# Layer 0 of a four-layer graph network: gathers three parts ahead instead of eight, ranks on ScalarE, early projections one part apart, last norms on ScalarE

## The chip, the cores and the metric

The kernel runs on one core of a Trainium2 chip. The metric is the time of one execution on the device, in microseconds (us). The engines are named as in the profile: PE (TensorE, matrix products), PEld (its weight loads), DVE (VectorE), ACT (ScalarE), POOL (GpSimd) and SP (SyncE, which here only issues DMAs). Each engine works through its own instructions in a fixed order and waits where an instruction needs the result, or the buffer, of another engine.

## The reference, cut to what matters

The input is a matrix x of 3327 nodes with 256 features and an adjacency matrix adj (int32, symmetric, about 1% ones, ones on the diagonal). Four graph attention layers follow one another, each with a residual and a layer norm:

```python
x = layernorm(x + L0(x, adj, ...))   # one head, score = a . leaky_relu(g_src[i] + g_tgt[j])
x = layernorm(x + L1(x, adj, ...))   # one head, score = leaky_relu(s1[i] + s2[j])
x = layernorm(x + L2(x, adj, ...))   # one head, score = s_src[i] + s_dst[j]
x = layernorm(x + L3(x, adj, ...))   # two passes of four heads of 64, leaky_relu, elu
return x
```

In each, a node's scores over its neighbours go through a softmax, and the weighted sum of the neighbours' projected rows is the layer's output. In layer 0 the leaky_relu is taken of a vector of 256 for every pair of neighbours, so it has no cheap product form. Layers 1 to 3 need only an outer sum of two columns.

## The kernel before, in words

The 3327 rows are 26 tiles of 128. **Layer 0 (sparse0)** works on the neighbours alone. The tiles form four groups of 4, 7, 9 and 6 tiles (SETS). For each group, `neighbours` finds the neighbours of its rows from the adjacency matrix: SP loads pieces of 1024 columns, ACT converts them to bf16 and counts the ones (`convert`, L543), PE adds column numbers, DVE takes the largest eight of each chunk (`scan`, L579), sorts them (`sort`) and writes them down (`note`, L599 and L606). Each row then gets a key from its number of neighbours (`turn_key`: ACT, PE, ACT), and its rank among the rows of the group is the number of keys above its own: one DVE operation per tile that compares all key rows of the group with the tile's keys and counts them (L678), then a conversion to integers, ranks_i (L682). With the ranks the rows are sorted by degree: POOL writes each tile's list of neighbours to its place (`write_list`, L731, one indirect DMA per tile), and reads the sorted lists back (`read_lists`, L739). Sorted tiles hold rows of like degree, so that a tile t gathers only as many neighbours as its largest row has (LEVELS), between 26 and 56.

The gathers of a tile are cut into **parts** of up to four neighbours, 237 parts in all; the groups begin at parts 0, 39, 102 and 182. For a part, POOL issues one indirect DMA per neighbour (`gather`, L912); each fetches 128 rows, one per partition, into one of 22 buffers g of four rows (TURNS). Before the first part of a tile, `gather_own` (L897) fetches the tile's own rows into one of four buffers. DVE scores the part (`score`: L932 takes the larger of two vectors for all four neighbours at once, L938 multiplies by the attention vector and adds up, once per neighbour). At a tile's last part DVE takes the largest score and ACT makes the weights. From the next step on ACT multiplies each gathered row by its weight (`combine`, L1012), and PE adds the rows up in PSUM (L1015). For the very last tile, all rows but those of four cuts are added on DVE instead (`add_aside`, L991 and L993). `add_input` (L1041, L1045, L1048, on DVE) divides by the sum of the weights and adds the residual, ten steps after the tile's last part, and `put_back` (L1057, on POOL) writes the tile's result to its unsorted place in DRAM. When a group is complete, `take` loads its rows back (DMAs issued by ACT), `finish_sums` makes means and variances on DVE, `finish_root` takes the root on POOL (L1097), and `finish` normalizes on DVE (L1106).

The order of the work of layer 0 is written out by hand. A loop over the parts q, called steps, does for each q: some units of `neighbours` of the next group, as many as are needed to have that group done by its due step (`owed`; `steps_of` says how many units a group has); then whatever is noted for step q (`due`, filled by `at_step`); then `gather(q + LEAD)`, with the gathers of own rows noted for it (`once_placed`); then `score(q)`. So LEAD, 8 parts, says how far POOL's gathers stand ahead in program order of the scores and of everything else that is noted for a step. `put_back` and `write_list` are appended to a list `between` and issued one after every second gather. The due step of a group's lists is its begin less LEAD, 2 and half its size and 1: with respect to POOL's gathers, `write_list` and `read_lists` stand at the same place for any LEAD, since the gathers move by LEAD too. Each engine's own queue holds only its own instructions, in this order; so between engines LEAD shows only where one waits for another.

Beside the gathers the projections of layer 1 for the first three groups are done early, tile by tile (`turn_next`, `project_next`, L1142 to L1170), one tile every two steps; those of the third group (group 2) begin 38 steps after the last group's first part, or later. They run through PE, ACT and stores on SP (L1160), and the last one ends with the rates of a block of tiles (L1164 to L1170).

**Layers 1 to 3** are dense: for each block of columns (7, 7, 6 and 6 tiles) a loop runs over the 26 source tiles j. DVE (layers 1 and 3) makes the unnormalized weights e of j by one operation per head (`weigh`, L1629), and PE multiplies them into accumulators (L1723, L1773, L1781). Layer 1 begins with what is left of layer 0: the last group's `take`, sums, root and norms (`last_group`) are worked off inside its first loop. Layer 3 is two such passes of four heads. What comes after a block is put in a list of pending work, and is worked off, a piece per j, inside the next block's loop. For the second pass that is `finish_last` (its `add` at L1947 to L1953): back to rows, elu, residual, moments, then `scaled` (L250 adds the epsilon on DVE, L251 takes the root on POOL, L257 normalizes tile by tile on DVE), then SP stores the rows to the output. After the last block this work stands at the kernel's end. `scaled` is also what `norms` calls in the other layers.

Of the kernel before, what the change touches and what calls it, by code (L numbers as in the profile page):

```python
# [8 lines left out]
F32 = mybir.dt.float32  # L9
# [10 lines left out]
P = 128  # L20
# [30 lines left out]
def gat_stack(  # L51
# [226 lines left out]
    def sparse0(lost):  # L278
        GROUP, TURNS, LEAD, SPREAD = 4, 22, 8, 8
        starts = [sum(SETS[:s]) for s in range(len(SETS))]  # L280
        with ExitStack() as s0:
# [238 lines left out]
            def steps_of(s):  # L520
                return SETS[s] * (len(banks_n) + 2) + 8

            def neighbours(s):
# [151 lines left out]
                yield  # L675
                for t in range(size):
                    junk = find.tile([P, max(SETS) * P], U16, tag="junk_r", name="junk2", bufs=1)
                    nc.vector.tensor_scalar(  # L678
                        junk[:, : size * P], key_rows[:, : size * P], keys[:, t : t + 1], 0.0,
                        op0=ALU.is_gt, op1=ALU.add, accum_out=ranks[:, t : t + 1],  # L680
                    )
                nc.vector.tensor_copy(ranks_i[:, :size], ranks[:, :size])  # L682
                placed[s] = ranks_i, payloads
# [547 lines left out]
            for q, key in ends.items():  # L1231
# [9 lines left out]
                if key[1] == SETS[key[0]] - 1 and key[0] < len(SETS) - 1:  # L1241
                    at_step(q + 21, take, key[0])
                    at_step(q + 27, finish_sums, key[0])
                    at_step(q + 33, finish_root, key[0])
                    at_step(q + 37, finish, key[0])
            for s, q in begins.items():
                work, at = excess(s), max(q - 2, 0)
                for y in range(12):
                    at_step(at + y, go_on, work)
# [4 lines left out]
            for s in range(len(SETS) - 1):  # L1254
                for it in range(starts[s], starts[s] + SETS[s]):
                    at_step(at, turn_next, it)
                    at_step(at + 2, project_next, it)
                    at += 2
                if s == len(SETS) - 3:
                    at = max(at, begins[len(SETS) - 1] + 38)  # L1260
            def keep_targets(s):
# [244 lines left out]
    def layers(rs, early=0, rest=None):  # L1506
# [402 lines left out]
        def finish_last(b, o, sums):  # L1909
# [45 lines left out]
            yield from staged([(s, s) for s in range(len(block))], [(0, back), (3, add)])  # L1955
            yield from scaled(block, [h[it] for it in block], mv)
            for it in block:
# [182 lines left out]
```

## Time and profile before

| What | Value |
| --- | --- |
| Time, median of 5 runs | 2954.26 us (2949.02 to 2961.05) |
| Profiled execution: time, span | 2954.82 us, 2953.0 us |
| Busy share of the span | PE 79%, DVE 72%, PEld 46%, POOL 34%, ACT 28% |
| Instructions | PE 15862, DVE 5634, ACT 2358, POOL 1061 |
| Mean granted clock of PE | 0.873 |
| Gathers (L912, POOL) | 894, 853.0 us busy, 954 ns each |
| First to last gather | about 86 to 1343 us |
| First matmul of layer 1 | 1365.85 us |
| Ranks (L678, DVE) | 26, 29.8 us busy, median 1146 ns |

The spans of the table are those of one profiled execution; the times of the profile's rows begin at the start of its span. A row of a group gives the line, the engine, the operation, the tensors (out<-in), the count, then the busy time in us and the mean in ns of one, then the idle time of the engine ahead of the group and what ended most of it. A row of a timeline gives the start in us, the busy time, and in brackets the idle time just before with its releaser. A row of waits gives the engine and line that waited, for which engine's result, and then the total in us, the number of times and the longest.

### The profile page before, as it was taken

The page shows a single profiled execution, that of the slowest core. Times are in us where ns is not written, and L with a number is a line of the kernel's source. Part 1 is how long each engine was busy: PE and PEld are TensorE (multiplying, and loading weights), DVE is VectorE, ACT ScalarE, POOL GpSimd, SP SyncE. Part 2 cuts the span into 40 slices and gives each one's busy share as a digit, 9 for nine tenths or more (in the row PEclk, how much of TensorE's full clock was granted, in tenths as well). Part 3 has the DMA queues.
Part 4 walks back from the last instruction along what each step waited for, and adds up shares of the span by engine and source line. Part 5 has one row for each costly group of instructions (what it writes and reads, how often), then busy time and mean ns, then how long its engine had stood idle before and what let it go on. Part 6 is the DMA issues. An engine that isn't in the chain of part 4 may idle for free. (4 is left out here: it accounts for less than half of the span.)

```text
span 2953.0 us, 45075 instructions
## 1 busy us (share of the span) xinstructions
PE 2318.7 (79%) x15862; PEld 1357.3 (46%) x15862; DVE 2140.2 (72%) x5634; ACT 840.6 (28%) x2358; POOL 994.1 (34%) x1061
## 2 busy tenths in 40 slices
PE   7466767556545416647899999999999999999997
PEld 4222323222222103325788888863556667534332
DVE  6789789968776528765455521138999999899997
ACT  4244445434334304543344311111010110110111
POOL 2676767777777777772000000000000000000000
PEclk8576777777767757889999999999999999999998
DMA  7684655445644435545766633331222222212211
GB/s 236 201 264 145 187 167 165 140 132 156 166 112 114 112 107 124 171 121 171 226 208 195 196 82 111 106 96 45 77 60 82 75 79 64 71 45 59 59 45 48
DMA packets 183854, 370.50 MB, mean 125 GB/s; under 512 B 35772, under 2 KB 124707, under 8 KB 182596
## 3 DMA queue, kind: packets, MB, share of 16 engines
q1 hardware_dynamic: 103994, 178.49, 21.0%
q0 software_dynamic: 51008, 155.70, 18.8%
q10 hardware_dynamic: 28618, 33.33, 3.2%
q8 instruction: 128, 2.10, 0.3%
q14 instruction: 106, 0.87, 0.1%
HBM read 327.52 MB, written 46.23 MB: 127 GB/s over the span
## 5 line engine op out<-in xcount | busy, mean ns | idle before, releaser
L912 POOL DMA_INDIRECT g<-table_d,lst x894 | 853.0, 954 | 273.0 <-issue 247.1
L1629 DVE SCALAR_TENSOR_TENSOR e<-rate,feat,at 128x896 f32<-128x896 f32 (+4 forms) x832 | 843.1, 1078 | 58.1 <-PE acc L1781 47.3
L1015 PE MATMUL acc<-g,ident 128*128 128x512 f32 (+1 forms) x896 | 505.5, 708 | 265.1 <-ACT g L1012 247.7
L1773 PE MATMUL acc<-e,feat 128*32 128x384 f32 (+2 forms) x6656 | 697.2, 515 | 6.4 <-DVE h L1745 3.4
L1773 PEld LDWEIGHTS acc<-e,feat 128*32 128x32 f32 x6656 | 307.0, 110 | 304.7 <-issue 159.0
L1015 PEld LDWEIGHTS acc<-g,ident 128*128 128x128 f32 x896 | 195.2, 228 | 483.3 <-ACT g L1012 365.6
L1781 PE MATMUL acc<-e,feat 128*32 128x384 f32 (+3 forms) x3328 | 383.2, 512 | 0.0
L1012 ACT ACTIVATE g<-g,w 128x256 f32<-128x256 f32 x883 | 365.5, 495 | 0.4 <-ACT minus L489 0.4
L932 DVE TENSOR_TENSOR y<-g,minus_ps 128x1028 f32<-128x1028 f32 (+2 forms) x233 | 273.2, 1173 | 126.4 <-DMA g<-table_d,lst 119.0
L938 DVE SCALAR_TENSOR_TENSOR y<-y,a_ps 128x257 f32<-128x257 f32 x894 | 324.5, 418 | 25.1 <-PE a_ps L781 5.8
L1723 PE MATMUL acc<-feat,e 128*128 128x257 f32 (+2 forms) x1352 | 303.9, 382 | 8.3 <-DVE inv L1744 5.7
L251 POOL TENSOR_TENSOR rstds<-rstds,minus_half 128x7 f32<-128x7 f32 (+1 forms) x12 | 19.7, 1643 | 773.9 <-DVE rstds L250 773.9
L1723 PEld LDWEIGHTS acc<-feat,e 128*128 128x128 f32 (+2 forms) x1352 | 254.9, 191 | 46.5 <-issue 8.6
L1723 PE MATMUL acc<-feat,at 128*128 128x257 bf16 (+2 forms) x2028 | 237.8, 274 | 4.1 <-DMA at<-at_d 3.9
L1781 PEld LDWEIGHTS acc<-e,feat 128*32 128x32 f32 (+1 forms) x3328 | 161.9, 110 | 130.7 <-issue 87.9
L1723 PEld LDWEIGHTS <-at 128*128 128x128 bf16 (+2 forms) x2028 | 198.8, 99 | 37.9 <-DMA at<-at_d 4.4
L553 PE MATMUL v<-code,leads 65*128 65x512 bf16 (+1 forms) x182 | 82.7, 456 | 155.7 <-DVE cand L579 121.9
L1629 DVE SCALAR_TENSOR_TENSOR e<-rate,feat,at_i 128x896 f32<-128x896 f32 (+2 forms) x104 | 112.2, 1080 | 90.8 <-DMA at_i<-in_adj_t_dram 43.1
L579 DVE MAX8 cand<-v 128x8 f32<-128x104 f32 (+2 forms) x858 | 158.6, 259 | 20.8 <-PE v L556 20.8
L1609 POOL DMA_DIRECT2D rate3b_d<-rate_rows x4 | 2.1, 520 | 450.5 <-ACT rate_rows L1608 450.5
L1656 ACT CAST at<-at_i 128x896 bf16<-128x896 int32 (+2 forms) x104 | 92.1, 885 | 112.5 <-DMA at_i<-in_adj_t_dram 75.6
L553 PEld LDWEIGHTS <-leads 65*128 65x128 bf16 x182 | 22.1, 121 | 191.1 <-DVE cand L579 161.2
(248 smaller groups left out, 1832.2 us busy)
## 6 DMA issues: line engine op xcount, KB each, us to landing
adj_i<-in_adj_dram SPq DMA_DIRECT2D x75, 512.0 KB
at<-at_d SPq DMA_DIRECT2D x150, 224.0 KB
at_i<-in_adj_t_dram SPq DMA_DIRECT2D x50, 448.0 KB
at<-at_d SPq DMA_DIRECT2D x75, 192.0 KB
at<-at_d SPq DMA_DIRECT2D x75, 191.8 KB
g<-table_d,lst POOLq DMA_INDIRECT x894, 2.8
at_d<-at ACTq DMA_DIRECT2D x50, 224.0 KB
at_i<-in_adj_t_dram SPq DMA_DIRECT2D x25, 384.0 KB
```

The lines of the kernel that those rows point to most:

```text
L553: nc.tensor.matmul(v[:, :w], leads[:, b, :], code[:, :w], start=True, stop=False)
L579: nc.vector.max(spread[:, c0 + c, :], view(v[:, :w]))
L912: nc.gpsimd.indirect_dma_start(out=g[:, k - k0, :], out_offset=None, in_=table_d[:, :], in_offset=bass.IndirectOffsetOnAxis(ap=entry["lst" ...
L932: nc.vector.tensor_tensor(y, rows, minus_src[:, None, :].to_broadcast([P, m, dim + 1]), op=ALU.max)
L938: nc.vector.scalar_tensor_tensor(y, y, 1.0, a_ps[:, : dim + 1], op0=ALU.mult, op1=ALU.mult, accum_out=sc)
L1012: nc.scalar.activation(rows, rows, AF.Copy, scale=w[:, k : k + 1])
L1015: nc.tensor.matmul(dst, ident, rows, start=start, stop=stop)
L1629: nc.vector.scalar_tensor_tensor(e[:pn, : c1 - c0], self.rate[b][:pn, h_of, : c1 - c0], q, at[:pn, : c1 - c0], op0=ALU.max, op1=ALU.mult,)
L1656: nc.scalar.copy(at[:pn, :w], at_i[:pn, :w])
L1723: nc.tensor.matmul(accs[s][:pn, : dim + 1], a[:pj, s * P : s * P + pn], f[:pj, : dim + 1], start=(j == 0 and part == 0), stop=(j == nt - 1 ...
L1773: nc.tensor.matmul(accs[x][p][q : q + 32, : hi - lo], f[:pj, at0 : at0 + 32], es[at0 // hd][:pj, lo:hi], start=(j == 0), stop=(j == nt - 1),)
L1781: nc.tensor.matmul(accs[x][pairs][h_of * 32 : (h_of + 1) * 32, : hi - lo], f[:pj, dim + h_of : dim + h_of + 1].to_broadcast([pj, 32]), es[ ...
```

## The change

Six things change. LEAD is 3 instead of 8. The later steps of a finished group come nearer to its last part: `take` after 17 steps instead of 21, `finish_sums` 21 instead of 27, `finish_root` 24 instead of 33, `finish` 27 instead of 37; the work on rows with more neighbours than seats (`excess`) begins one step before the group instead of two. The ranks of groups 1 to 3 are made by ACT: the sign of (key row minus key plus a half), added up, two tiles per unit of `neighbours`, and one DVE operation turns the sums into integers; `steps_of` counts these units. The buffer of the compared rows is bf16 there. Group 0's ranks stay on DVE. The early projections of group 2 stand one step apart instead of two, and begin 28 steps after the last group's first part instead of 38. In `finish_last`, the norms are done by ACT, as scale and shift, with one more DVE operation per block for the shifts; in the last block every second tile's norm stays on DVE. After the change, LEAD being 3, a group's lists are due five steps later in the order than before, `add_input` still stands ten steps after the tile's last part, and `put_back` thirteen.

```diff
--- before.py
+++ after.py
@@ -276,7 +276,7 @@
 
 
     def sparse0(lost):
-        GROUP, TURNS, LEAD, SPREAD = 4, 22, 8, 8
+        GROUP, TURNS, LEAD, SPREAD = 4, 22, 3, 8
         starts = [sum(SETS[:s]) for s in range(len(SETS))]
         with ExitStack() as s0:
             find = s0.enter_context(tc.tile_pool(name="s_find", bufs=2))
@@ -518,7 +518,7 @@
             listed = {}
 
             def steps_of(s):
-                return SETS[s] * (len(banks_n) + 2) + 8
+                return SETS[s] * (len(banks_n) + 2) + 8 + ((SETS[s] + 1) // 2 if s else 0)
 
             def neighbours(s):
 
@@ -673,13 +673,35 @@
                     turn_key(size - 1, stage)
                 yield
                 yield
-                for t in range(size):
-                    junk = find.tile([P, max(SETS) * P], U16, tag="junk_r", name="junk2", bufs=1)
+                if s == 0:
+                    for t in range(size):
+                        junk = find.tile(
+                            [P, max(SETS) * P], U16, tag="junk_r", name="junk2", bufs=1
+                        )
+                        nc.vector.tensor_scalar(
+                            junk[:, : size * P], key_rows[:, : size * P], keys[:, t : t + 1], 0.0,
+                            op0=ALU.is_gt, op1=ALU.add, accum_out=ranks[:, t : t + 1],
+                        )
+                    nc.vector.tensor_copy(ranks_i[:, :size], ranks[:, :size])
+                else:
+                    below_key = io0.tile([P, max(SETS)], F32, tag="keys", name="below_key")
+                    nc.scalar.activation(
+                        below_key[:, :size], keys[:, :size], AF.Copy, bias=-0.5, scale=-1.0
+                    )
+                    for t in range(size):
+                        junk = find.tile(
+                            [P, max(SETS) * P], BF16, tag="junk_r", name="junk2", bufs=1
+                        )
+                        nc.scalar.activation(
+                            junk[:, : size * P], key_rows[:, : size * P], AF.Sign,
+                            bias=below_key[:, t : t + 1], accum_out=ranks[:, t : t + 1],
+                        )
+                        if t % 2 or t == size - 1:
+                            yield
                     nc.vector.tensor_scalar(
-                        junk[:, : size * P], key_rows[:, : size * P], keys[:, t : t + 1], 0.0,
-                        op0=ALU.is_gt, op1=ALU.add, accum_out=ranks[:, t : t + 1],
-                    )
-                nc.vector.tensor_copy(ranks_i[:, :size], ranks[:, :size])
+                        ranks_i[:, :size], ranks[:, :size], 0.5, size * P / 2 + 0.25,
+                        op0=ALU.mult, op1=ALU.add,
+                    )
                 placed[s] = ranks_i, payloads
                 if s == 0:
                     permute(size, ranks, ranks_i, payloads)
@@ -1239,12 +1261,12 @@
                 at_step(q + 10, add_input, *key)
                 at_step(q + 13, between.append, lambda key=key: put_back(*key))
                 if key[1] == SETS[key[0]] - 1 and key[0] < len(SETS) - 1:
-                    at_step(q + 21, take, key[0])
-                    at_step(q + 27, finish_sums, key[0])
-                    at_step(q + 33, finish_root, key[0])
-                    at_step(q + 37, finish, key[0])
+                    at_step(q + 17, take, key[0])
+                    at_step(q + 21, finish_sums, key[0])
+                    at_step(q + 24, finish_root, key[0])
+                    at_step(q + 27, finish, key[0])
             for s, q in begins.items():
-                work, at = excess(s), max(q - 2, 0)
+                work, at = excess(s), max(q - 1, 0)
                 for y in range(12):
                     at_step(at + y, go_on, work)
             at = begins[len(SETS) - 1]
@@ -1255,9 +1277,9 @@
                 for it in range(starts[s], starts[s] + SETS[s]):
                     at_step(at, turn_next, it)
                     at_step(at + 2, project_next, it)
-                    at += 2
+                    at += 2 if s < len(SETS) - 2 else 1
                 if s == len(SETS) - 3:
-                    at = max(at, begins[len(SETS) - 1] + 38)
+                    at = max(at, begins[len(SETS) - 1] + 28)
             def keep_targets(s):
                 lo, hi = starts[s] * P, min(n, (starts[s] + SETS[s]) * P)
                 copy_rows(nc.sync, own_d[s][: hi - lo, AT_TGT:], table_d[1 + lo : 1 + hi, :])
@@ -1953,7 +1975,31 @@
                 nc.vector.bn_aggr(mv[:pn, s, :], stats[:pn])
 
             yield from staged([(s, s) for s in range(len(block))], [(0, back), (3, add)])
-            yield from scaled(block, [h[it] for it in block], mv)
+            rstd = small.tile([P, len(block)], F32, tag="rstds", name="rstds")
+            shift = small.tile([P, len(block)], F32, tag="rstds", name="shifts")
+            nc.vector.tensor_scalar(rstd, mv[:, :, 1], EPS, None, op0=ALU.add)
+            nc.gpsimd.tensor_tensor(
+                rstd, rstd, minus_half.to_broadcast([P, len(block)]), op=ALU.pow
+            )
+            yield
+            nc.vector.scalar_tensor_tensor(
+                shift, mv[:, :, 0], -1.0, rstd, op0=ALU.mult, op1=ALU.mult
+            )
+            for s, it in enumerate(block):
+                pn = rows_of(it)
+                if b == len(blocks) - 1 and s % 2:
+                    nc.vector.tensor_scalar(
+                        h[it][:pn], h[it][:pn], mv[:pn, s, 0:1], rstd[:pn, s : s + 1],
+                        op0=ALU.subtract, op1=ALU.mult,
+                    )
+                else:
+                    nc.scalar.activation(
+                        h[it][:pn], h[it][:pn], AF.Identity,
+                        bias=shift[:pn, s : s + 1], scale=rstd[:pn, s : s + 1],
+                    )
+                if s == len(block) // 2:
+                    yield
+            yield
             for it in block:
                 pn = rows_of(it)
                 copy_rows(nc.sync, out[it * P : it * P + pn, :], h[it][:pn])
```

## The prediction

> **What bounds the kernel now.** I read the slices of the page first, to see which engine is full when, then the largest groups, then POOL's waits while it gathers, then the timelines at the seams.
>
> ```profile
> PE   7466767556545416647899999999999999999997
> DVE  6789789968776528765455521138999999899997
> POOL 2676767777777777772000000000000000000000
> L912 POOL DMA_INDIRECT g<-table_d,lst x894 | 853.0, 954 | 273.0 <-issue 247.1
> ```
>
> A slice is 73.8 us. From slice 2 to slice 18 POOL shows a steady 7, PE and DVE go up and down; from slice 20 on PE shows 9. So there are two regimes: layer 0 and the dense layers. POOL's 7 is a full queue: a gather is busy for 954 ns and the next starts 0.30 us later ("issue", a gap that the profile puts down to no other engine), 1.26 us from start to start. At that pace 100 us hold 79.5 gathers. Windows of 100 us (PE, PEld, DVE, ACT, POOL busy, then clock):
>
> ```profile
> 200.00:300.00 100.00, 64.87 (x162) 28.64 (x160) 94.92 (x403) 47.41 (x126) 66.68 (x70) 0.73 0.59 177
> 900.00:1000.00 100.00, 48.47 (x91) 21.27 (x92) 59.38 (x207) 37.69 (x98) 75.92 (x80) 0.72 0.41 112
> ```
>
> At 900 POOL issues 80, nothing is missing, and DVE at 59% has room. At 200 it issues 70: DVE is at 95% and POOL waits for it. A gather not issued then is never caught up, so in layer 0 only POOL's longer waits cost time. All of those above 1 us between 100 and 1300 us:
>
> ```profile
> POOL g L912 <- PE acc L1015: 10.5, 32, 1.1
> POOL own_of L897 <- DVE hs L1041: 10.4, 1, 10.4
> POOL lists_d L731 <- DVE ranks_i L682: 9.1, 1, 9.1
> POOL own_of L897 <- DVE y_over L845: 3.1, 1, 3.1
> ```
>
> Beyond the usual 0.30 us gap these single waits are 10.1, 8.8, 2.8 and (the 1.1) 0.8: 22.5 us. The sum is made against the profiled execution: 2954.82 us, of which 2953.0 are the span and 1.82 lie around it; it is 0.56 above the median of 2954.26. What a measurement of this kernel can tell from no change is about 0.2%, 5.9 us.
>
> **Part 1, three parts ahead, and the ranks: the end of the gathers.** Reads of lists, writes of lists and the gathers of own rows keep their places among POOL's gathers. What moves on POOL is the put_back of a tile (now 16 parts after the tile's last gather, before 21) and the root of a group (now ahead of the gather 27 parts on, before 41). On DVE each step now stands behind five more scores as seen from POOL.
>
> The write of group 1's lists. In before the last note of group 1 ends at 243.4; ACT's key, PE's row and ACT's copy follow, and then seven ranks on DVE:
>
> ```profile
> 249.93 0.27 ACT L627 COPY key_rows<-key_row 128x128 f32<-128x128 f32 x1 [3.90 <-PE key_row L623]
> 255.29 1.05 ACT L543 ACTIVATE adj_b<-adj_i 128x1024 bf16<-128x1024 int32 x1
> 256.33 1.04 ACT L543 ACTIVATE adj_b<-adj_i 128x1024 bf16<-128x1024 int32 x1
> 261.02 1.00 POOL L731 DMA_INDIRECT lists_d<-payload,ranks_i  x1 [9.14 <-DVE ranks_i L682]
> ```
>
> The new order puts three more scores before that note; with what leaves, DVE's work up to it adds up, in start-to-start intervals of the trace, to 144.5 instead of 136.2 us: the note ends at 251.7. Key, row and copy take the 6.5 us of before (243.4 to 250.2): 258.2. Then seven ranks on ACT. There is no row for a rank there; the nearest is the accumulating conversion of 1024 columns, 1.04 from start to start, so 0.91 by width for 896 columns and 1.04 at most; seven take 6.4 to 7.3. Between their pairs stand some 12 scalings of gathered rows at 0.40 (4.8). ranks_i comes at 258.2 + 6.9 + 4.8 = 269.9. POOL reaches its first write at 252.2 less the 3.6 of the two short stalls, which go because DVE reaches those scores sooner in its order: 248.6. It waits 21 us where it waited 8.8 + 3.6.
>
> The own row's 10.1 us. POOL waits there for DVE's add_input of tile (0,3), which frees the buffer. DVE had 122.0 us of work and 19.8 us of waits between ranks_i and it; in the new order the work is 94.0, so with the same waits it is done at 269.9 + 113.8 = 383.7, and POOL, which came at 392.5 and has now waited 8.6 us more, comes at about 401. This stall goes. Next late are the moved instructions: put_back of (1,1) behind gather 64 needs another 53.5 us of DVE's work and 1.4 of waits, 438.6, and POOL is there at 435.4 (3.3 us); the root of group 0 ahead of gather 65 finds its sums 2.9 us late. Later groups find theirs ready: by then DVE idles in front of nearly each score for gathers. Sum of POOL's waits: 21 + 3.3 + 2.9 = 27.3 against 22.5: **+4.8 us**. Ends: −6.2 if ACT takes the ranks with no scaling between them (4.8 less) and DVE waits 6.2 us less in this stretch, so that the two last stalls go (27.3 − 11.0 = 16.3); +12 if the ranks find ACT behind by two more runs of eight scalings (3.3 each, 6.6 more). I keep the middle, since each of its terms has a row. DVE's 60 us of waits for put_back and 32 for the root after 1000 us shrink; POOL bounds there, so 0; without that cover, by the bound of those waits, they would be worth tens of us.
>
> The other 15 ranks off DVE (15 x 1.19 = 18 us) and two small operations per group more: 0, since POOL is full in these stretches and DVE at 59%. The Trainium skill, "Perfetto Trace Analysis", "Identifying the Most-Contended Engine", says to optimize the engine with the highest occupancy first; in the window at 200 that is DVE, so by it all 22 ranks (26 us) would come off the time; in the window at 900 POOL, busy 76%, is full all the same for its gaps, and only what it waits for counts. The skill's "ScalarE: Activation LUTs", "What ACT_TABLE_LOAD costs", speaks against the ranks on ACT: it gives 2.66 us for each switch of table set, and if Sign and Exp needed different sets, eight switches around group 1's ranks would add some 21 us by an estimate from that page; no row here shows a switch.
>
> **Part 2, group 2's projections one part apart.** They now end some 18 parts before the last gather. In before they cross the tail:
>
> ```profile
> 1350.73 3.28 ACT L1012 ACTIVATE g<-g,w 128x256 f32<-128x256 f32 x8
> 1359.12 0.17 ACT L1153 ACTIVATE feat<-early 128x1 f32<-128x1 f32 x1 [5.10 <-PE early L452]
> 1360.05 3.29 ACT L1012 ACTIVATE g<-g,w 128x256 f32<-128x256 f32 x8
> 1361.00 3.70 PE L1015 MATMUL acc<-g,ident 128*128 128x512 f32 x8 [1.15 <-ACT g L1012]
> 1365.85 15.41 PE L1723 MATMUL acc<-feat,e 128*128 128x257 f32 x70 [1.15 <-issue]
> ```
>
> ACT ends eight scalings at 1354.0, waits 5.10 us for the last projection, spends 0.9 on it, and only then scales the last eight rows. Without that they run from 1354.0 to 1357.3, and PE adds them as soon as its four adds of before end at 1358.0: done at 1361.7 instead of 1364.7. DVE's side sum for that tile ends at 1359.5, so it doesn't take over. hs, its put_back, the first loads of layer 1 (SP waits 8.7 us for that put_back) and the first matmul follow: **−3.0 us**, and PE is full behind it. Ends −1 (SP's stores late) and −3.3.
>
> **Part 3, the last norms on ACT.** In layer 3's second pass a j of a block of seven takes PE 4.51 us; DVE needs 4.25 for its four weighings and has 0.17 to spare. A block's norms of before stand in the next block's j's:
>
> ```profile
> 2588.31 4.34 DVE L1629 SCALAR_TENSOR_TENSOR e<-rate,feat,at 128x896 f32<-128x896 f32 x4 [0.17 <-PE acc L1781]
> 2655.75 1.38 DVE L257 TENSOR_SCALAR h<-h,mvs,rstds 128x256 f32<-128x256 f32 x4
> 2657.05 4.33 DVE L1629 SCALAR_TENSOR_TENSOR e<-rate,feat,at 128x896 f32<-128x896 f32 x4
> 2661.30 1.05 DVE L257 TENSOR_SCALAR h<-h,mvs,rstds 128x256 f32<-128x256 f32 x3
> ```
>
> Four norms add 1.30, three 0.97: j's of 5.54 and 5.22 instead of 4.51, 1.74 us over. In the block of six columns PE needs 3.87 and the same norms give 1.96, in the last (six norms) 1.63. ACT is nearly idle there (slices of 1). Gain **−5.3 us**. Ends: −6.5 if DVE has no slack at all and each norm's time comes back (2 x 2.27 + 1.95), −3.5 if the new shift operation (0.2) and a wait for it take 0.6 per block.
>
> **Part 4, the kernel's end.** The last block splits six norms between ACT and DVE; the stores on SP, about 0.45 us each, set the end: 0, ends −0.3 and +0.3.
>
> **Sum:** +4.8 − 3.0 − 5.3 = −3.5; 2954.82 − 3.5 = **2951.3 us**. All good ends: −6.2 − 3.3 − 6.5 − 0.3 = −16.3, 2938.5; all bad ends: +12 − 1 − 3.5 + 0.3 = +7.8, 2962.6.
>
> **Rivals.** (a) *The gathers end no later*: ACT is at 47% around the ranks, and the stalls of 10.1, 2.8 and 0.8 go whatever the ranks do. Against it: a rank on ACT starts only after DVE's note, 8.3 us late. Then part 1 is 0 to −6.2, the time 2940.3 to 2946.5: faster. (b) *Slower: POOL waits for DVE at the moved put_backs and the root.* DVE is at 95% up to 500 us, and a put_back five parts sooner takes away 25 us of DVE's leave. If DVE comes 10 us later to gather 64 than I count, part 1 is near +15 and all of it about 2961.5; it is slower than before from +8.3 and past the measurement from +14.2. Against it: the 28 us of ranks and scores that leave this stretch on DVE. (c) *The norms were hidden*: PE could make good a longer j out of its buffers of e, and parts 2 and 4 alone are left: −3.0 + 4.8, 2956.6, the same. Against it: DVE's spare 0.17 per j refills nothing. (d) *The change does nothing*: its steps only swap places under POOL's full queue: 2954.8. Against it: the 5.10 us in the tail.
>
> **How the numbers follow.** My sum 0.40 (of it 0.15 faster by over 0.2%, 0.22 within, 0.03 slower), (a) 0.25 faster, (b) 0.18 slower, (c) 0.13 (0.11 within, 0.02 slower), (d) 0.04 (0.02 within, 0.02 faster). Faster 0.42, same 0.35, slower 0.23. The range takes in all good ends and (b) at its price: 2938.5 to 2963, the bad ends' sum with it; the likeliest case's own is 2946 to 2957.
>
> **What would show it.** Right: a first write of lists at about 270 with a wait of 21 us on POOL, no long wait at own rows near 400, waits of about 3 us at gathers 64 and 65, a last gather near 1347, ACT's last eight scalings directly after the eight before, no norms on DVE in the last pass but three. Wrong: a last gather past 1355 or before 1342, or DVE still behind PE in the j's where ACT norms.

## The result, and the profile after

The changed kernel takes 2956.28 us (median of 25 runs, 2948.76 to 2963.20), the kernel before 2955.86 us (47 runs, 2948.69 to 2962.42). The ratio is 1.000, with a 95% interval of 0.9994 to 1.0006: no difference, or at most 1.8 us either way. The forecast was 2951.3 us, 3.5 us less than before.

The profiled execution of the changed kernel took 2952.54 us, with a span of 2950.7 us. That is 3.7 us under its median, where the profiled execution of before was 1.0 us under its own; so of the 2.3 us by which the two profiles differ, 2.7 us less is only where these two executions lie among the others. What the two profiles can tell is where time went and came from, seam by seam (starts in us, from the timelines):

| Seam | before | after | stretch changed by |
| --- | --- | --- | --- |
| first gather | 86.98 | 86.83 | −0.2 |
| last gather | 1342.17 | 1349.58 | +7.6 |
| first matmul of layer 1 | 1365.85 | 1369.42 | −3.8 |
| first weighing, layer 3, second pass, block 0 | 2445.04 | 2448.02 | −0.6 |
| the same, block 1 | 2568.49 | 2571.47 | 0.0 |
| the same, block 2 | 2696.97 | 2698.05 | −1.9 |
| the same, block 3 | 2811.12 | 2810.31 | −1.9 |
| end of its last weighing | 2922.61 | 2920.23 | −1.6 |
| end of the span | 2953.04 | 2950.67 | 0.0 |

Between these two profiles the change gains in two places, 3.8 us in the tail of layer 0 and 5.4 us in the last pass, and loses in one, 7.6 us of gathers. The slices of the page after show no new shape, and the gathers go at 952 ns (954 before) with the same gap:

```profile
PE   7466667555553536657899999999999999999997
L934 POOL DMA_INDIRECT g<-table_d,lst x894 | 851.1, 952 | 277.8 <-issue 249.8
```

**The gathers.** POOL's waits between 100 and 1300 us (engine and line that waited, for what; total us, times, longest):

```profile
POOL lists_d L753 <- DVE ranks_i L701: 16.3, 1, 16.3
POOL g L934 <- DMA g<-table_d,lst: 11.7, 23, 3.5
...
POOL rstd L1119 <- DVE rstd L1114: 3.1, 1, 3.1
POOL sums_d L1079 <- PE v L556: 2.9, 1, 2.9
```

Against the list of before, the wait of 10.4 us at own rows is gone, and so are the two short ones. The write of lists waits 16.3 us instead of 9.1. Three new waits stand at what was moved: two put_backs and the root. A fourth, of 3.5 us, stands at nothing that was moved: a gather that, by the profile, waited for an earlier gather of POOL's to land. On POOL's timeline the four and the write are these: that gather; the put_back of tile (0,1), whose add_input ends on DVE at 215.8 (the profile puts the wait down to PE); the write; the put_back of tile (1,1), behind the gathers of part 64; the root of group 0:

```profile
203.44 0.95 POOL L934 DMA_INDIRECT g<-table_d,lst  x1 [3.46 <-DMA g<-table_d,lst]
...
216.12 1.01 POOL L1079 DMA_INDIRECT sums_d<-hs,lst  x1 [2.93 <-PE v L556]
...
271.20 1.00 POOL L753 DMA_INDIRECT lists_d<-payload,ranks_i  x1 [16.33 <-DVE ranks_i L701]
...
441.27 1.00 POOL L1079 DMA_INDIRECT sums_d<-hs,lst  x1 [1.71 <-DVE hs L1070]
...
447.91 1.05 POOL L1119 TENSOR_TENSOR rstd<-rstd,minus_half 128x4 f32<-128x4 f32 x1 [3.10 <-DVE rstd L1114]
```

The own rows at which POOL waited, behind the 214th of its gathers into g in both kernels, before and after:

```profile
402.61 0.95 POOL L897 DMA_INDIRECT own_of<-own_d,lst  x1 [10.37 <-DVE hs L1041]
```

```profile
405.91 0.95 POOL L919 DMA_INDIRECT own_of<-own_d,lst  x1 [0.31 <-issue]
```

ACT's side of the write: the key at 251.19, the copied row at 256.48, then seven ranks (L695) with fourteen scalings ahead of and between them. Two ranks in a row start 1.17 us apart. DVE, which turns the sums into integers, waits 7.07 us for the last rank, so ACT sets the time of this write:

```profile
256.48 0.27 ACT L627 COPY key_rows<-key_row 128x128 f32<-128x128 f32 x1 [2.97 <-PE key_row L623]
256.64 3.30 ACT L1034 ACTIVATE g<-g,w 128x256 f32<-128x256 f32 x8
...
260.07 1.04 ACT L695 ACTIVATE junk<-key_rows,below_key 128x896 bf16<-128x896 f32 x1
...
261.24 1.04 ACT L695 ACTIVATE junk<-key_rows,below_key 128x896 bf16<-128x896 f32 x1
...
270.75 0.17 DVE L701 TENSOR_SCALAR ranks_i<-ranks 128x7 uint32<-128x7 f32 x1 [7.07 <-ACT junk L695]
```

The write starts 10.2 us later than before. Of these, 6.5 us are there when the copied row is (it ends at 250.20 before and at 256.75 after), and 3.6 come between that row and the write, where ACT now makes the ranks.

**The tail.** ACT's last sixteen scalings of rows now follow one another without a wait, and PE's last adds too:

```profile
1357.36 6.48 ACT L1034 ACTIVATE g<-g,w 128x256 f32<-128x256 f32 x16
1362.97 5.31 PE L1037 MATMUL acc<-g,ident 128*128 128x512 f32 x12
1369.42 15.76 PE L1745 MATMUL acc<-feat,e 128*128 128x257 f32 x71 [1.14 <-issue]
```

From hs of the last tile but one to hs of the last it took 12.15 us (1352.59 to 1364.74) and takes 9.10 (1359.22 to 1368.32): 3.05 us. The other 0.8 is a shorter way from the last gather's issue to that first hs (10.42 and 9.64 us); why it is shorter is not shown.

**The last norms.** In the block whose norms are finished inside the next one, DVE has one small operation where seven norms stood, and ACT does the seven beside it:

```profile
2654.13 4.33 DVE L1651 SCALAR_TENSOR_TENSOR e<-rate,feat,at 128x896 f32<-128x896 f32 x4
2658.38 0.15 DVE L1985 SCALAR_TENSOR_TENSOR shifts<-mvs,rstds 128x7 f32<-128x7 f32 x1
2658.45 13.89 DVE L1651 SCALAR_TENSOR_TENSOR e<-rate,feat,at 128x896 f32<-128x896 f32 x13
2658.57 3.55 ACT L1996 ACTIVATE h<-h,shifts,rstds 128x256 f32<-128x256 f32 x7 [21.14 <-DVE shifts L1985]
```

For the numbers that follow: on the chips of the experiments the kernel before itself took 3379 to 3402 us, since there the engines often stop for some us in layer 0 (and only there), so every ratio below is to the kernel before on the same chip, and no size in us of layer 0 is carried over from there to the result above.

### The profile page after: what moved, and what is told of

It is laid out like the page before. It is cut to its first block, busy times and chain, and to the rows that moved or that the text cites. A ratio compares the mean times of both kernels' runs of the same rounds, so it can differ in the third digit from the quotient of the medians.

```text
span 2950.7 us, 45070 instructions
## 1 busy us (share of the span) xinstructions
PE 2329.1 (79%) x15862; PEld 1361.9 (46%) x15862; DVE 2110.5 (72%) x5571; ACT 877.7 (30%) x2428; POOL 992.1 (34%) x1061
## 5 line engine op out<-in xcount | busy, mean ns | idle before, releaser
L1037 PE MATMUL acc<-g,ident 128*128 128x512 f32 (+1 forms) x896 | 517.6, 721 | 347.2 <-ACT g L1034 288.3
L1745 PEld LDWEIGHTS acc<-feat,e 128*128 128x128 f32 (+2 forms) x1352 | 255.2, 191 | 45.5 <-issue 8.4
```

The costliest lines, as they stand in the source:

```text
L1037: nc.tensor.matmul(dst, ident, rows, start=start, stop=stop)
L1745: nc.tensor.matmul(accs[s][:pn, : dim + 1], a[:pj, s * P : s * P + pn], f[:pj, : dim + 1], start=(j == 0 and part == 0), stop=(j == nt - 1 ...
```

## The experiments

In each, what isn't named is as in the kernel before, and in experiments 5 to 8 as in the changed kernel. Sums of POOL's waits are those of its gaps over 0.4 us between the first and the last gather, less the usual 0.30 each. No profile of the kernel before was taken on these chips; experiment 1, whose layer 0 is that of before, stands in for it.

**1. The norms alone**

```diff
-            yield from scaled(block, [h[it] for it in block], mv)
+            shift = small.tile([P, len(block)], F32, tag="rstds", name="shifts")
...
+                    nc.scalar.activation(
+                        h[it][:pn], h[it][:pn], AF.Identity,
+                        bias=shift[:pn, s : s + 1], scale=rstd[:pn, s : s + 1],
+                    )
```

> The kernel before with the norms of the last pass on ScalarE and nothing else. My theory: each of the three later blocks of the second pass of layer 3 gets shorter by what VectorE's norms stood over PE's own pace, 1.7, 2.0 and 1.6 us; the gathers and layers 1 and 2 stay where they are; the time falls by 5.3 us (0.18%). Rival, the norms were hidden: PE makes good the two longer j's, the blocks keep their lengths and the time stays within 1 us.

Measured: ratio 0.9982 (0.9961 to 1.0003). The runs alone can't tell it from no change, the timeline can, since layers 1 to 3 run undisturbed on this chip: the three blocks take 126.94, 112.28 and 109.94 us instead of 128.48, 114.15 and 111.49 in the profile of before: −1.54, −1.87 and −1.55, together −5.0 us of 5.3 expected. The second kernel below, which has before's norms, shows 128.50, 114.16 and 111.51 on the same chip. DVE of this kernel:

```profile
3108.59 4.33 DVE L1629 SCALAR_TENSOR_TENSOR e<-rate,feat,at 128x896 f32<-128x896 f32 x4
3112.84 0.16 DVE L1963 SCALAR_TENSOR_TENSOR shifts<-mvs,rstds 128x7 f32<-128x7 f32 x1
3112.91 9.64 DVE L1629 SCALAR_TENSOR_TENSOR e<-rate,feat,at 128x896 f32<-128x896 f32 x9
```

The rival, hidden norms, falls.

**2. The early projections alone**

```diff
-                    at += 2
+                    at += 2 if s < len(SETS) - 2 else 1
                 if s == len(SETS) - 3:
-                    at = max(at, begins[len(SETS) - 1] + 38)
+                    at = max(at, begins[len(SETS) - 1] + 28)
```

> The kernel before with group 2's projections one step apart and 28 steps after the last group's begin, nothing else. My theory: from the start of the last gather to the first matmul of layer 1 it takes 20.0 to 20.7 us instead of 23.7, ScalarE's last sixteen scalings of rows have no wait between them, and the time falls by 3.0 to 3.8 us (0.10 to 0.13%). Rival, SyncE's stores of these projections or the loads of layer 1 hold its start: less than 1 us.

Measured: ratio 0.9974 (0.9960 to 0.9989), a gain of 0.26%. From the last gather to the first matmul of layer 1 it takes 42.6 us, and 62.5 us in the kernel of experiment 1, which has before's projections: 20 us, far more than the 3 to 3.8 expected. The whole time fell by less, 9 us (4 to 14 by the interval); where the rest went is not shown. ACT at the end of layer 0, here and then there:

```profile
1788.74 0.89 ACT L1012 ACTIVATE g<-g,w 128x256 f32<-128x256 f32 x2
1789.54 0.49 ACT L1012 ACTIVATE own_of<-own_of,w 128x256 f32<-128x256 f32 x1
1789.93 6.48 ACT L1012 ACTIVATE g<-g,w 128x256 f32<-128x256 f32 x16
```

```profile
1785.05 0.17 ACT L1153 ACTIVATE feat<-early 128x1 f32<-128x1 f32 x1 [2.58 <-PE early L452]
...
1785.88 3.30 ACT L1012 ACTIVATE g<-g,w 128x256 f32<-128x256 f32 x8
1791.45 0.17 ACT L1153 ACTIVATE feat<-early 128x1 f32<-128x1 f32 x1 [2.27 <-PE early L452]
...
1792.28 3.30 ACT L1012 ACTIVATE g<-g,w 128x256 f32<-128x256 f32 x8
1797.86 0.17 ACT L1153 ACTIVATE feat<-early 128x1 f32<-128x1 f32 x1 [2.27 <-PE early L452]
```

With projections two steps apart, each of the last ones costs ACT a wait of 2.3 us ahead of eight scalings. In the profile of before ACT had all but one of them behind it at the end of the gathers; here ACT comes late, several stand in line, and the change is worth more. The mechanism is the same, the size depends on how far ACT is behind.

**3. Lead and nearer steps alone** (the ranks still on DVE), run on three chips

```diff
-        GROUP, TURNS, LEAD, SPREAD = 4, 22, 8, 8
+        GROUP, TURNS, LEAD, SPREAD = 4, 22, 3, 8
...
-                    at_step(q + 21, take, key[0])
-                    at_step(q + 27, finish_sums, key[0])
-                    at_step(q + 33, finish_root, key[0])
-                    at_step(q + 37, finish, key[0])
+                    at_step(q + 17, take, key[0])
+                    at_step(q + 21, finish_sums, key[0])
+                    at_step(q + 24, finish_root, key[0])
+                    at_step(q + 27, finish, key[0])
...
-                work, at = excess(s), max(q - 2, 0)
+                work, at = excess(s), max(q - 1, 0)
```

> The kernel before with the gathers three parts ahead and the nearer steps of a group, the ranks still on VectorE. My theory, in which the order alone makes group 1's ranks late (three more scores ahead of the last note): the first write of group 1's lists at 268 to 271 us instead of 261.0, no long wait at own rows near 400 us, waits of 1 to 4 us at gathers 64 and 65, the last gather starting at 1346 to 1350 us instead of 1342.2, the time 4 to 8 us longer. Rival, ScalarE's ranks make the write late: then with VectorE's ranks it comes at 261 to 264 us and the last gather starts at 1335 to 1339 us.

> The kernel before with the gathers three parts ahead and the nearer steps of a group alone, once more: the first time all engines stalled many times in layer 0 on that chip, in the kernel before too, and the time was 3.7% longer. Theory, without such stalls: the first write of group 1's lists at 268 to 271 us, no long wait at own rows near 400 us, the last gather 4 to 8 us later than before, the time 4 to 8 us longer (0.15 to 0.3%). Rival, the lead costs as much here: 3% or more.

> The kernel before with three parts of lead and the nearer steps of a group alone, beside the run with eight, to split the changed kernel's 7.4 us later last gather between lead and ranks on a chip without stalls. Theory: the lead makes all of it, the last gather at 1346 to 1350 us, first write at 268 to 271 us. Rival, the ranks on ScalarE make it: last gather at 1335 to 1340 us. If engines stall here too: 3.5 to 4% slower, as on the first two chips (3.67 and 3.81%).

Measured: ratios 1.0367 (1.0340 to 1.0395), 1.0381 (1.0359 to 1.0404) and 1.0375 (1.0355 to 1.0396). The theory's numbers for a chip without stalls could not be tried, and the question that was put, whether lead or ranks make the 7.6 us of the result, stays open. The loss of 3.7 to 3.8% is far larger than theory or rival of the first run had; it is what the second run's rival (3% or more) and the third's forecast for such a chip (3.5 to 4%) said. POOL's waits at put_back grow from 132 us (experiment 1) to 429, 417 and 443 us. POOL's waits in the first of these runs:

```profile
POOL sums_d L1057 <- DVE hs L1048: 373.0, 18, 41.7
POOL g L912 <- issue: 262.4, 859, 1.3
POOL lists_d L731 <- DVE ranks_i L682: 61.3, 2, 42.4
```

**4. The ranks alone**, run on two chips

```diff
+                    for t in range(size):
...
+                        nc.scalar.activation(
+                            junk[:, : size * P], key_rows[:, : size * P], AF.Sign,
+                            bias=below_key[:, t : t + 1], accum_out=ranks[:, t : t + 1],
+                        )
+                        if t % 2 or t == size - 1:
+                            yield
```

> The kernel before with the ranks of groups 1 to 3 on ScalarE, gathers eight parts ahead as before. My theory: note at 243.4 us as before, then 6.5 us for key and row and 11.7 for seven ranks among scalings, so the first write at about 262 us (1 us later than before); VectorE has 8.3 us less to do ahead of add_input of tile (0,3), so the wait of 10.4 us at own rows falls below 3 us; the last gather starts at 1333 to 1337 us, the time falls by 6 to 9 us. Rival, only the smaller lead removes the wait at own rows: it stays at 8 us or more, and the last gather within 2 us of 1342.2.

> The kernel before with only the ranks of groups 1 to 3 on ScalarE, once more, for the same reason. Theory, without the stalls: the first write of group 1's lists at about 262 us, the wait of 10.4 us at own rows below 3 us, the last gather at 1333 to 1337 us, the time 6 to 9 us shorter (0.2 to 0.3%). Rival: the wait at own rows stays and the time is within 2 us.

Measured: ratios 0.9924 (0.9899 to 0.9950) and 0.9940 (0.9916 to 0.9963), a gain of 0.6 to 0.8%, more than the 0.2 to 0.3% forecast. The first write waits 4.3 us at 338.8 us instead of 9.4 at 343.7 in experiment 1, and the sum of POOL's waits is 396 and 397 us instead of 443. So the ranks on ACT alone don't make the write late here; they take work off the engine that POOL waits for. The forecast wait at own rows stands later here, at the same place in POOL's order (behind the 214th gather), and the ranks on ACT don't touch it: it is 21.3 us in experiment 1 and 21.7 in both runs of this kernel. In the changed kernel, experiment 5, and in the three runs of experiment 3 it is the usual gap. In order, experiments 1, 4 and 5:

```profile
547.16 0.95 POOL L897 DMA_INDIRECT own_of<-own_d,lst  x1 [21.30 <-DVE hs L1041]
```

```profile
532.71 0.96 POOL L919 DMA_INDIRECT own_of<-own_d,lst  x1 [21.71 <-DVE hs L1063]
```

```profile
552.59 0.95 POOL L919 DMA_INDIRECT own_of<-own_d,lst  x1 [0.30 <-PE acc L1037]
```

So on these chips the rival is right about this wait: it goes with the smaller lead and not with the ranks. That POOL has by then lost more time at the nearer put_backs fits this: with three parts of lead and later put_backs (experiment 7) it is 13.8 us again. The gain of the ranks lies elsewhere, at put_back (93 and 87 us instead of 132) and at the writes of lists (19 and 16 instead of 36).

**5. The changed kernel itself**

> The changed kernel itself, beside the kernel before on one chip, to see whether the chip decides. Theory A (three parts of lead are too few where all engines stall at once): on a chip with such stalls the waits at put_back are 4 to 5 times those of the kernel before, and the time is 2 to 4% longer; on a chip without them the time is within 0.15% of before, the last gather starts 5 to 8 us later than with eight parts, and the rest is 8 to 9 us shorter. Theory B (the ranks on ScalarE make up for the smaller lead): within 0.5% of before on either chip.

Measured: ratio 1.0390 (1.0370 to 1.0410). Theory A has the size (2 to 4%); theory B, that the ranks make up for the lead, falls here. The waits at put_back are 447 us, 3.4 times those of experiment 1 (A had 4 to 5). POOL's waits:

```profile
POOL sums_d L1079 <- DVE hs L1070: 356.8, 16, 41.1
POOL g L934 <- issue: 262.6, 858, 1.3
POOL sums_d L1079 <- DVE seat L822: 51.6, 2, 26.1
```

The tail (39.9 us, 62.5 in experiment 1) and the last pass (472.2 us from its first to its last weighing, 472.2 in the profile of the result, 477.6 before) are as short as they should be; the whole loss is in the gathers, 1796 us from first to last against 1670 in experiment 1.

**6. The changed kernel with eight parts of lead**, run on two chips

```diff
-        GROUP, TURNS, LEAD, SPREAD = 4, 22, 3, 8
+        GROUP, TURNS, LEAD, SPREAD = 4, 22, 8, 8
```

(the steps of a group and of `excess` are those of before, too)

> The changed kernel with eight parts of lead and the group's steps of before; ranks, early projections and last norms as changed. My theory: each of the three gains by itself and they add up: the last gather starts 6 to 9 us earlier than in the kernel before, the tail is 3 to 3.8 us shorter and the last pass 5.3 us: 14 to 18 us (0.5 to 0.6%) faster than before where engines don't stall, 1% where they do (the ranks alone gave 0.8% there). Rival: the smaller lead is what removes the wait at own rows, so without it the gathers end where they did and only 8 to 9 us are gained.

> The changed kernel with eight parts of lead and the steps of before, once more, since engines stalled in layer 0 on the chip of its first run. Theory, without stalls: the first write of group 1's lists at about 262 us, the wait at own rows near 400 us below 3 us, the last gather at 1333 to 1337 us, 14 to 18 us (0.5 to 0.6%) faster than before. Rival: the wait at own rows needs the smaller lead; the last gather at 1341 to 1344 us, 8 to 9 us faster. If engines stall here too: 0.5 to 1.0% faster, as on the first chip (0.73%).

Measured: ratios 0.9927 (0.9907 to 0.9947) and 0.9876 (0.9854 to 0.9899): 0.7 and 1.2% faster than before, the second a little more than expected. On the chip of experiment 5 it is 4.4% faster than the changed kernel (3357.77 against 3513.61 us). So it beats the kernel before on both chips, and the changed kernel on the one where both ran. That it beats the ranks alone is not shown: on that chip the intervals of the two ratios (0.9907 to 0.9947 here, 0.9916 to 0.9963 there) overlap. The wait at own rows is still 21.3 and 21.7 us, as its rival said, though more is gained than the rival's 8 to 9 us. Where the engines don't stop so often, as in the result, this kernel wasn't run.

**7. The changed kernel with later put_backs**

```diff
-                at_step(q + 13, between.append, lambda key=key: put_back(*key))
+                at_step(q + 18, between.append, lambda key=key: put_back(*key))
...
-                    at_step(q + 17, take, key[0])
-                    at_step(q + 21, finish_sums, key[0])
-                    at_step(q + 24, finish_root, key[0])
-                    at_step(q + 27, finish, key[0])
+                    at_step(q + 22, take, key[0])
+                    at_step(q + 24, finish_sums, key[0])
+                    at_step(q + 26, finish_root, key[0])
+                    at_step(q + 28, finish, key[0])
```

> The changed kernel, three parts of lead and all, but with each tile's put_back noted five steps later, so that it stands behind the same gather as in the kernel before (take, sums, root and norms of a group follow at 22, 24, 26 and 28 steps). Theory A, the place of put_back in GpSimd's queue is what three parts of lead cost where engines stall: the waits at put_back fall from some 370 to 390 us to 130 at most and the time comes within 1% of before (after was 3.9% over it). Rival, something else of the order costs it (ranks late, scores nearer the gathers): the time stays 2.5% or more over before. On a chip whose engines don't stall, theory A: the 1.4 us wait at put_back goes, the last gather starts 1 to 3 us earlier than in the changed kernel's profile (1349.6), and the time is within 0.1% of it.

Measured: ratio 1.0145 (1.0121 to 1.0169), between the two bounds. The waits at put_back fall from 447 to 114 us, below the 132 of experiment 1, as theory A says. Three fifths of the loss is back, not all of it:

```profile
POOL rstd L1119 <- DVE rstd L1114: 95.1, 3, 39.0
POOL sums_d L1079 <- DVE hs L1070: 83.0, 8, 18.0
...
POOL lists_d L753 <- DVE ranks_i L701: 60.4, 2, 32.7
```

The root now takes 94 us (9 to 10 in the kernels with three parts of lead above, 0 in experiment 1), and the writes of lists 64 (50 in the changed kernel, 36 in experiment 1). The root is no nearer than in the changed kernel: it stands 29 parts after a group's last gather here, 27 there and 41 in the kernel before. But its sums are noted three steps later than there, two steps ahead of it and not three, and POOL no longer loses the time at put_back ahead of it; which of the two makes the 94 us is not shown. So the cost is not that of one step alone: put_back takes the largest share, and what no longer waits there waits in part at the next of POOL's instructions that need DVE's work.

**8. Eight parts of lead and later put_backs**

```diff
-                at_step(q + 13, between.append, lambda key=key: put_back(*key))
+                at_step(q + 18, between.append, lambda key=key: put_back(*key))
...
-                    at_step(q + 21, take, key[0])
+                    at_step(q + 22, take, key[0])
```

(against number 6)

> Eight parts of lead, ranks, early projections and last norms as changed (the kernel of the second set that was 0.7% faster than before), and each put_back five steps later still, so that it stands behind the gather 26 parts after the tile's last (before: 21; changed kernel: 16). Theory A, each step of distance between put_back and add_input takes waits from GpSimd for good: the waits at put_back fall from 111 us to below 50 and the last gather starts 20 us or more earlier than without this (1719.8), the time is 1.2% or more below before. Rival, the waits only move on to own rows and to the ring of gathered rows, since VectorE paces layer 0 where the engines stall: the sum of GpSimd's waits while it gathers stays within 20 us of 408, and the time at 0.5 to 0.9% below before. Where engines don't stall both expect 0.5 to 0.6% below before and a first write at about 262 us.

Measured: ratio 0.9891 (0.9869 to 0.9913), between the ratios of number 6. No wait at put_back is left, and POOL waits as long as before, elsewhere: 413.7 us in all against 408.0, at own rows 192 (160) and at the ring of gathered rows 209 (119). The rival is right: once POOL stands far enough from its put_backs, more distance moves the wait and doesn't remove it. Number 6 and this one are the same within what the runs tell.

```profile
POOL g L934 <- PE acc L1037: 124.0, 23, 14.3
POOL own_of L919 <- DVE hs L1063: 65.8, 6, 21.7
POOL own_of L919 <- DVE y_over L867: 45.0, 3, 20.1
```

## Why the prediction was right or wrong

**The sum.** That gains and a loss of like size nearly cancel held, and the time lies in the range, and in the likeliest case's own (2946 to 2957). The forecast gain of 3.5 us is not there: by the interval the change lies between −1.8 and +1.8 us, inside what I had called within the measurement and had given 0.35, less than the 0.42 for faster. Three slips of the sum change nothing: 243.4 to 250.2 is 6.8 us and not 6.5, the waits 21, 3.3 and 2.9 make 27.2 and not 27.3, and 4.8 and 6.6 make 11.4 for the bad end of 12.

**Part 3, the last norms**: −5.3 forecast, −5.4 in the profile after (−1.9, −1.9, −1.6 against −1.74, −1.96, −1.63), −5.0 by themselves in experiment 1. Each term held. Rival (c) is excluded.

**Part 2, the tail**: −3.0 forecast, −3.05 from hs to hs in the profile after. PE's adds, not ACT's scalings, set the end, as the sum had it. Experiment 2 confirms the mechanism, and shows that its size is a matter of how late ACT is.

**Part 4, the kernel's end**: 0 forecast, 0.0 found.

**Part 1, the gathers**: this is the term that was mis-sized, +4.8 forecast and +7.6 in the profile after. Its steps one by one:
- The first write of lists, forecast at about 270, came at 271.20. That it is so near is luck in part; on the way to it three errors nearly cancel: the key row was there 1.5 us sooner (256.7 for 258.2), fourteen scalings stood among the ranks and not twelve (0.8), and a rank costs 1.17 us from start to start, not 0.98 (1.3 for seven): the conversions of 1024 columns, which start 1.04 us apart, were too cheap a neighbour; why a rank, narrower and as long (1.04 us), is followed later is not shown. The wait was 16.3 us and not 21, only because POOL came late itself.
- It came there at 255.2 and not 248.6, by waits that I had left out. The put_back of tile (0,1) is also moved five parts nearer, and waits 2.6 us beyond the gap; I had counted the moved put_backs from the write on. And two gathers, at 199.02 and 203.44, wait 3.7 us beyond it for earlier gathers to land. Both fall into the wait for the ranks and cost the end nothing by themselves.
- The wait at own rows went, as forecast (POOL passes there at 405.91, some 5 us later than forecast, with its usual gap of 0.31). Put_back at gather 64: 1.4 us beyond the gap for 3.3; root of group 0: 2.8 for 2.9.
- These alone make +4.3: the write 10.2 us later than before, less 10.1, plus 1.4 and 2.8. The rest, some 3 us, is the net of POOL's small waits after the write: for its own DMAs to land (1.24 and 0.44 us beyond the gap at group 1's lists, 1.56 at the reading of group 2's), 0.53 at the lists that the profile puts down to ACT, and one gap of 1.3 us that it ascribes to nothing. I had them at the value of before, 0.9 in all; this is what was sized too small. That they belong to the new order, and not to this one execution, is not shown.

**The runs against the profiles**: the two profiles differ by 2.3 us, the medians by 0.4 the other way, and an execution differs from the next by up to 14 us. Where the changed kernel's other executions are slower than the profiled one can't be read from one profile; that it is the gathers is likely, but not shown.

**Rival (b)**, POOL waiting for DVE at the moved put_backs and the root, named the right places. In the result they weigh 4.2 us behind the write (1.4 and 2.8), less than the 6.2 of the sum itself and far from the 10 more that the rival was priced at; the 2.6 ahead of the write fall into its wait. Its premise of a DVE at 95% up to 500 us was too high: the windows of before show 86% from 100 to 200 us and 77% from 300 to 400. Where DVE is often late these waits decide the time (experiments 3, 5 and 7), and I gave them the price of one stall of DVE and not of one per put_back. **Rival (a)** falls with a last gather 7.4 us later, **rival (d)** with the seams.

**The two rules of pages.** The Trainium skill, "Perfetto Trace Analysis", "Identifying the Most-Contended Engine", says to optimize the engine with the highest occupancy first. Read as the prediction read it, the 26 us of ranks taken off DVE should have come off the time; in the result no such gain is left, though there the ranks don't stand alone. In experiment 4 they gained 0.6 to 0.8%, and there it is the waits that say so and not the busy share: between the first and the last gather of experiment 1, DVE is busy for 932 us and POOL for 933 of 1670. The skill's "ScalarE: Activation LUTs", "What ACT_TABLE_LOAD costs", prices a switch of table set at 2.66 us. The profile after has one table load in the whole execution, as before, so Sign and Exp shared a set and no switch came:

```profile
4.57 1.28 ACT L543 ACT_TABLE_LOAD   x1 [4.57 <-DMA adj_i<-in_adj_dram]
```

## What to carry to other kernels

A change that does several things at once can gain and lose in different stretches and end at nothing: read it seam by seam, and then keep the parts apart. Distance in program order between an engine's instruction and the work it waits for pays when one of the two is late: taking five parts of it away, with the steps of a group nearer too, cost 3.7 to 3.8% where DVE was often late (experiment 3). What it is worth where both keep pace was not measured by itself. Take it away only from steps whose waits the trace shows to be over long before, and count every such step on the queue, the first tile's too. Past the point where such a wait is gone, more distance only moved it to the next shared buffer (experiment 8).

## What the runs showed of the hardware

On the chips of the experiments engines stopped again and again between the first and the last gather, and not before or after: the first gather starts at 83 to 88 us in each kernel, as in the result, and layers 1 to 3 take the same time to within some us. In between, a gather's own time is unchanged (median 948 ns in experiment 1, 949 before), but DVE waits long for things that it has itself just made. In the result's profile each of the 338 steps of a search (L587 and the loads of L589) follows its predecessor, on the same engine, after 34 ns. In experiment 5, 60 of them come later, most often 1.1 us (18) or 2.5 us (16) after it, while POOL goes on issuing a gather every 1.26 us:

```profile
133.51 0.27 DVE L587 MAX8 found<-cand 128x8 f32<-128x107 f32 x1 [8.81 <-remote]
134.91 0.09 DVE L589 MATCH_VALUE_LOAD cand<-found,cand 128x8 f32 x1 [1.12 <-DVE found L587]
134.98 0.25 DVE L589 MATCH_REPLACE8 cand<-found,cand 128x107 f32<-128x107 f32 x1
137.71 0.27 DVE L587 MAX8 found<-cand 128x8 f32<-128x107 f32 x1 [2.47 <-remote]
139.12 0.09 DVE L589 MATCH_VALUE_LOAD cand<-found,cand 128x8 f32 x1 [1.14 <-DVE found L587]
```

DVE's waits of more than 2 us that the profile puts down to nothing or to "remote", a releaser outside it, are 405 us in experiment 1 (79 of them) between the first and the last gather, and 6 us in the profile of before (2). For ACT they are 395 and 0 us, for PE 362 and 18, for POOL 55 and 0. What makes the engines stop there, and whether it goes by the chip or by the time, stays open; no run tried it.
